# Spectral results of both signs in one store, sent one a step, in a fused attention and spectral-filter kernel

## The chip, the cores and the metric

The kernel runs on one core of one Trainium2 chip. The metric is the device time of one execution in microseconds (us). One execution was also recorded by the hardware profiler; its times are used wherever a single operation is priced.

## What is computed

The reference runs a convolutional-attention hybrid of two layers on x of shape (2, 128, 64, 64), in float32.

- Layer 0: group norm, then neighbourhood attention over 7x7 windows with four heads, two small dense layers with layer norms, and residuals.
- Layer 1, first half: the image as 4096 tokens of 128 features, layer norm, and full self-attention in which queries, keys and values are the same tokens and the diagonal is masked.
- Layer 1, second half: layer norm, then a spectral filter. Sixteen filters are convolved causally with the tokens by FFT, for the sequence as it is and for the sequence with alternating signs; the results are mixed by 128x128 matrices. Four branches of different length are combined by weights that in effect pick one branch. Three short lags of the sequence are added.

Cut to what matters here:

```python
t = _to_tokens(x)
t = t + _L1_attn_ref(_ln_t(t))          # softmax(q q^T / sqrt(128)), diagonal masked
t = t + _L1_ffn_ref(_ln_t(t), ...)      # the spectral filter
...
Uf_p = jnp.fft.rfft(u, n=n, axis=1)
Uf_m = jnp.fft.rfft(u * sgn3, n=n, axis=1)
U_plus  = jnp.fft.irfft(Vf[None, :, :, None] * Uf_p[:, :, None, :], n=n, axis=1)[:, :sl]
U_minus = jnp.fft.irfft(Vf[None, :, :, None] * Uf_m[:, :, None, :], n=n, axis=1)[:, :sl]
out = einsum('btkd,k,kde->bte', U_plus, s, Mpp) + einsum('btkd,k,kde->bte', U_minus, s, Mpm)
```

## The kernel before, in words

The program has four stretches. From 0 to about 350 us it computes layer 0. From 350 to about 770 us it computes the self-attention of batch 0, from 770 to about 1220 that of batch 1. From about 1220 to 1290 it finishes the last forward transforms and the short lags. From there on it runs the filter network for both batches: bursts of small matmuls make products of transformed tokens and filters (line 1570), these are projected by the mixing matrices (line 1589), and inverse transforms come in between (lines 1628 and 1670).

**Attention.** The tokens of a batch form 8 chunks of 512. `attention` walks the 36 pairs of chunks (a, c) with c >= a, four steps a pair. In a step TensorE multiplies keys with queries into a bank (line 927), ScalarE takes the exponential into a tile `e` (line 932, or 943 on the diagonal), and TensorE multiplies the exponentials with the tokens (`other`, line 1057). The same exponentials are needed transposed for the other chunk of the pair. A pair away from the diagonal sends them to DRAM with one 1 MB store issued by ScalarE (`eb`, line 959), SyncE fetches them back in blocks two steps later with four loads of 256 KB (`et`, line 966), VectorE turns 32x32 blocks in place (line 975), and TensorE uses them a few steps later (`own`, line 985). Within batch 1, and in batch 0 from the point where a tile exists, the order of each engine's queue is the order in which the program was written.

**The filler.** Each step of `attention` ends with one call of `fill()`. It first calls `stores()`, then advances one generator by one piece: one from the list `urgent` if there is one, or else one from the list `steps`. A generator that yields None ends the call; one that yields True passes the call on to the other list. `urgent` holds a chain `after(b, c)` for each chunk whose attention is complete, and the short lags. `steps` holds background work: for batch 0 the end of layer 0, the branch weights, the transforms of the filters (`filters`) and the tokens of batch 1; for batch 1 what was left over, and then `for_ffn`, which opens the memory of the network, mixes the 2 x 16 matrices of the four branches (`filter_matrices`), loads the inverse table `inv` (320 KB, SyncE, line 1502), scales it on VectorE (line 1504), and loads the first four sets of blocks and inputs (`load_blocks`).

**A chain.** `after` transposes the attention result of a chunk, divides by the denominator, adds the residual, normalizes (statistics, then apply), and makes the forward transform: 160 bins, of which a row tile holds 128 (real and imaginary part one after the other) and a left-over tile 32. For each of these three parts the function `store` copies two PSUM banks to SBUF (`uo`, ScalarE, line 1141, two buffers), forms sum and difference (`ub`, GpSimd, line 1144, four buffers; VectorE at the very end), and leaves DRAM stores to be issued: for a row tile one of 128 KB for each sign and each of two banks, for the left-over tile one of 32 KB for each sign, bank and half. A chain thus makes 8 large and 8 small stores, and there are 16 chains.

**The stores.** They go to the DRAM array `us`, and those of the filters to `gs` (through the same tag `ub` of four buffers). `store` only appends to the list `fresh_`. Each call of `stores()` issues on ScalarE's queue (line 1095) all that was appended up to the call before the last:

```python
def stores():
    for to, src in behind_:
        nc.scalar.dma_start(out=to, in_=src)
    behind_[:] = fresh_
    fresh_.clear()
```

In the network `inputs` loads from `us` (SyncE, line 1470, 128 KB, one load a burst, 160 in all), and `blocks` loads from `gs` (SyncE, line 1462, four loads a burst). Four bursts are loaded ahead. TensorE's order there is fixed by hand; a burst comes every 4.32 us.

Of the kernel before, what the change touches and what calls it, by code (L numbers as in the profile page):

```python
# [14 lines left out]
P = 128  # L15
# [87 lines left out]
def kernel(  # L103
# [767 lines left out]
    left_row, left_col = Q // P * P, 2 * (Q // P) * P  # L871


    us = dram.tile([Q, 2, 2, SG, FB, NB, 2, P], F32, name="us")
    gs = dram.tile([Q, 2, 2, SG, GROW], F32, name="gs")

    with ap_:
# [208 lines left out]

        spare = [tok[0][:, 0:4, :]]
        adder = [nc.gpsimd]
        behind_ = []

        fresh_ = []

        def stores():
            for to, src in behind_:
                nc.scalar.dma_start(out=to, in_=src)  # L1095
            behind_[:] = fresh_
            fresh_.clear()


        def after(b, c):  # L1100
# [36 lines left out]
            def store(pu, n, r0, m, ri):  # L1137

                for s in range(2):
                    both = sp.tile([P, 512], F32, tag="uo", name="uo", bufs=2)  # L1140
                    nc.scalar.copy(both[:, 0 : 2 * n], pu[s][:, 0 : 2 * n])  # L1141
                    ub = sp.tile([P, 2, 256], F32, tag="ub", name="ub", bufs=4)
                    for sgn, op in enumerate((ALU.add, ALU.subtract)):
                        adder[0].tensor_tensor(ub[:, sgn, 0:n], both[:, 0:n], both[:, n : 2 * n], op)  # L1144
                    for sgn in range(2):
                        to = us[r0 : r0 + m, sgn, :, 2 * hh + s, 2 * fp : 2 * fp + 2, b, par, :]
                        if ri is not None:
                            fresh_.append((to[:, ri], ub[:, sgn, :].rearrange("p (f d) -> p f d", d=P)))
                            continue
                        for f in range(2):  # L1150
                            fresh_.append((to[:, :, f].rearrange("k i d -> i k d"), ub[64 * f : 64 * f + 64, sgn, 0:P]))

            for r0, c0 in row_tiles:
                for ri in range(2):
                    pu = [bank() for _ in range(2)]
                    for e in range(2):
                        for s in range(2):
                            rows_ = slice(s * 64, (s + 1) * 64)
                            nc.tensor.matmul(  # L1159
                                pu[s][:, e * 256 : (e + 1) * 256], lhsT=tr[rows_, hh, e, c0 + ri * P : c0 + (ri + 1) * P],  # L1160
                                rhs=z[rows_, 2 * e : 2 * e + 2, :].rearrange("p f d -> p (f d)"), start=True, stop=True,
                            )
                    store(pu, 256, r0, P, ri)
                    if FB == 4 or ri:
                        yield

            pu = [bank() for _ in range(2)]
            for e in range(2):
# [6 lines left out]
                        )  # L1175
            store(pu, P, left_row, 32, None)
            yield

            if borrowed:
                spare.append(None)  # L1180
# [139 lines left out]
        def filters():  # L1320
# [24 lines left out]
            def store(src, r0, n, ri, s, i, o):  # L1345
                to = bass.AP(
                    gs.tensor, gs.offset + r0 * 4 * SG * GROW + (i * SG + s) * GROW + o * LL,
                    [[4 * SG * GROW, n], [2 * SG * GROW, 2], [1, LL]],
                )
                fresh_.append((to, src))  # L1350

            everything = [(r0, c0 + ri * P, (ri,), P) for r0, c0 in row_tiles for ri in range(2)]
            everything.append((left_row, left_col, (0, 1), 64))
            for r0, c0, parts_, m in everything:
                places = cm[1][:, SG * LL : (3 * SG) * LL].rearrange("p (j e c) -> p j e c", j=SG, e=2)
                for j in range(SG):
                    hh, a = divmod(j, 2)
                    if a == 0:
                        pf = [bank() for _ in range(2)]
                        for e in range(2):  # L1360
                            for s in range(2):
                                rows_ = slice(s * 64, (s + 1) * 64)
                                nc.tensor.matmul(
                                    pf[s][0:m, e * LL : (e + 1) * LL], lhsT=tr[rows_, hh, e, c0 : c0 + m],
                                    rhs=ph[hh, e][rows_].rearrange("p l f k -> p (l f k)"), start=True, stop=True,
                                )
                    sums = places[:, j]
                    whole, before = (places[:, i].rearrange("p e c -> p (e c)") for i in (j, max(j - 1, 0)))
                    if j == 0:
                        nc.scalar.copy(whole[0:m], pf[a][0:m, 0 : 2 * LL])  # L1370
                    else:
                        nc.vector.tensor_tensor(whole[0:m], pf[a][0:m, 0 : 2 * LL], before[0:m], ALU.add)
                    fb = sp.tile([P, 2, LL], F32, tag="ub", name="fb", bufs=4)
                    for sgn, op in enumerate((ALU.add, ALU.subtract)):
                        nc.gpsimd.tensor_tensor(fb[0:m, sgn, :], sums[0:m, 0, :], sums[0:m, 1, :], op)
                    n = m // len(parts_)
                    s = SG - 1 - j
                    for at, ri in enumerate(parts_):
                        mine = slice(at * n, (at + 1) * n)
                        store(fb[mine], r0, n, ri, s, 0, ri)  # L1380
                        if ri == 0:
                            store(fb[mine], r0, n, ri, s, 1, 1)
                    if 1 in parts_:
                        mine = slice(m - n, m)
                        fn = sp.tile([P, 2, LL], F32, tag="ub", name="fn", bufs=4)
# [9 lines left out]
        def filler(b, steps, kept=None):  # L1395

            urgent, done = [], []

            def fill(c=None):
                if c is not None:  # L1400
# [66 lines left out]
        def inputs(b, q):  # L1467

            ut = utp.tile([P, 2, P], F32, tag="ut", name="ut")
            nc.sync.dma_start(  # L1470
                out=ut.rearrange("p s d -> p (s d)"),
                in_=us[2 * q : 2 * q + 2, :, :, :, :, b].rearrange("g n i r f s d -> (g n i r f) (s d)"),
            )
# [11 lines left out]
        def for_ffn():  # L1485
# [9 lines left out]
            inv = l1.tile([P, K2 // BC * 4 + 1, CQ], F32, name="inv")  # L1495
            ctp = ctx.enter_context(tc.tile_pool(name="blocks", bufs=5))
            nc.gpsimd.tensor_copy(mu1, mu)
            with tc.tile_pool(name="mix", bufs=2) as mixp:
                yield from filter_matrices(mpl, mmi, mixp)
            utp = ctx.enter_context(tc.tile_pool(name="inputs", bufs=4))  # L1500

            nc.sync.dma_start(out=inv, in_=nc.inline_tensor(t_out, "t_out").ap().rearrange("(a p) c -> p a c", p=P))
            for s, (lo, hi) in enumerate(((0, CQ // 8), (CQ // 8, CQ // 4), (CQ // 4, CQ // 2), (CQ // 2, CQ))):
                nc.vector.tensor_scalar(inv[:, :, lo:hi], inv[:, :, lo:hi], seg[:, s : s + 1], None, ALU.mult)
            yield
# [355 lines left out]
```

## Time and profile before

| | |
|---|---|
| runs | 2048.33, 2054.34, 2054.42 us; median 2054.34 |
| profiled execution | 2047.53 us, span 2045.8 us, mean granted TensorE clock 0.975 |
| busy in the span | PE 1928.6 us (94%), DVE 942.2 (46%), ACT 728.9 (36%), POOL 598.2 (29%) |
| DMA | 225.97 MB in 262,698 packets; queue 1 (SyncE) 202,050 packets, 127.18 MB; queue 10 (ScalarE) 57,022 packets, 84.26 MB |
| stores to `us` | 128 of 128 KB and 128 of 32 KB, all from ScalarE |
| loads from `us` | 160 of 128 KB, all from SyncE |

PE is TensorE's matmul, PEld its weight load, DVE is VectorE, ACT is ScalarE, POOL is GpSimd, SP is SyncE; ACTq and SPq are the issues of transfers on those engines' queues. "Idle before" is the time that an engine stood before an instruction, and the releaser is what ended it. An instruction stands in the queue of its engine behind all that was written before it, so a wait of one is a wait of all behind it. The granted clock is the share of full speed that TensorE was given.

### The profile page before, as it was taken

The page shows a single profiled execution, that of the slowest core. Times are in us where ns is not written, and L with a number is a line of the kernel's source. Part 1 is how long each engine was busy: PE and PEld are TensorE (multiplying, and loading weights), DVE is VectorE, ACT ScalarE, POOL GpSimd, SP SyncE. Part 2 cuts the span into 40 slices and gives each one's busy share as a digit, 9 for nine tenths or more (in the row PEclk, how much of TensorE's full clock was granted, in tenths as well). Part 3 has the DMA queues.
Part 4 walks back from the last instruction along what each step waited for, and adds up shares of the span by engine and source line. Part 5 has one row for each costly group of instructions (what it writes and reads, how often), then busy time and mean ns, then how long its engine had stood idle before and what let it go on. Part 6 is the DMA issues. An engine that isn't in the chain of part 4 may idle for free. (4 is left out here: it accounts for less than half of the span.)

```text
span 2045.8 us, 50912 instructions
## 1 busy us (share of the span) xinstructions
PE 1928.6 (94%) x20504; PEld 1361.0 (67%) x20504; DVE 942.2 (46%) x2918; ACT 728.9 (36%) x1718; POOL 598.2 (29%) x990
## 2 busy tenths in 40 slices
PE   6899998999998999998987997999999999999998
PEld 4577775444444444443433444999999999999987
DVE  5799996453544344343452345333333333333332
ACT  3788885322222223222231322222222322222222
POOL 4467887303422113103311120122221122222211
PEclk8999999999999999999998997999999999999999
DMA  4222221667656534648765622222222223222211
GB/s 152 62 62 60 62 60 40 189 147 247 183 151 190 148 110 147 177 134 238 225 191 148 179 76 79 74 66 68 65 68 57 52 75 85 68 66 68 65 42 43
DMA packets 262698, 225.97 MB, mean 110 GB/s; under 512 B 122607, under 2 KB 223615, under 8 KB 255040
## 3 DMA queue, kind: packets, MB, share of 16 engines
q1 hardware_dynamic: 202050, 127.18, 25.5%
q10 hardware_dynamic: 57022, 84.26, 11.5%
q0 software_dynamic: 3392, 11.27, 2.0%
q8 instruction: 163, 2.67, 0.5%
q14 instruction: 71, 0.58, 0.1%
HBM read 131.40 MB, written 91.25 MB: 109 GB/s over the span
## 5 line engine op out<-in xcount | busy, mean ns | idle before, releaser
L1575 DVE COPY y<-pc 128x512 f32<-128x512 f32 x320 | 206.2, 686 | 348.2 <-PE pc L1570 347.9
L1589 PE MATMUL acc<-y,mpl 32*128 32x256 f32 x5120 | 324.6, 381 | 0.8 <-DVE af L1599 0.8
L1589 PE MATMUL acc<-y,mmi 32*128 32x256 f32 x5120 | 315.5, 375 | 0.0
L1575 ACT COPY y<-pc 128x512 f32<-128x512 f32 x320 | 171.8, 589 | 393.0 <-PE pc L1570 388.1
L1589 PEld LDWEIGHTS acc<-y,mpl 32*128 32x128 f32 x5120 | 290.1, 186 | 7.9 <-DVE af L1599 1.8
L1589 PEld LDWEIGHTS acc<-y,mmi 32*128 32x128 f32 x5120 | 291.0, 185 | 2.9
L985 PE MATMUL own<-et,tok 128*128 128x512 f32 x448 | 221.3, 618 | 28.7 <-DVE et L975 23.6
L1057 PE MATMUL other<-e,tok 128*128 128x512 f32 x448 | 234.0, 604 | 6.7 <-DVE xa L1066 6.5
L932 ACT ACTIVATE e<-bank 128x512 f32<-128x512 f32 x216 | 127.7, 600 | 283.2 <-PE bank L927 229.4
L927 PE MATMUL bank<-cm 128*128 128x512 f32 x432 | 224.7, 602 | 1.1 <-ACT xa L1192 1.1
L1600 POOL TENSOR_TENSOR af<-af 128x512 f32<-128x512 f32 x39 | 49.7, 1275 | 599.0 <-DVE af L1599 599.0
L1570 PE MATMUL pc<-ct,ut 32*128 32x256 f32 x2560 | 210.9, 378 | 2.1 <-DVE y L1575 2.1
L985 PEld LDWEIGHTS own<-et,tok 128*128 128x128 f32 x448 | 85.7, 196 | 142.8 <-issue 101.2
L1570 PEld LDWEIGHTS pc<-ct,ut 32*128 32x128 f32 x2560 | 172.2, 187 | 8.0 <-DVE y L1575 4.2
L975 DVE STREAM_TRANSPOSE et<-et 128x1024 f32<-128x1024 f32 x108 | 127.7, 1220 | 75.9 <-DMA et<-eb 67.9
L1144 POOL TENSOR_TENSOR ub<-uo 128x256 f32<-128x256 f32 (+1 forms) x160 | 97.1, 638 | 183.1 <-ACT uo L1141 157.7
L1057 PEld LDWEIGHTS other<-e,tok 128*128 128x128 f32 x448 | 82.4, 194 | 99.5 <-issue 81.6
L174 POOL TENSOR_TENSOR ln_rs<-ln_rs,mhalf 128x4 f32<-128x4 f32 x24 | 25.4, 1056 | 346.4 <-DVE ln_rs L173 346.4
L927 PEld LDWEIGHTS bank<-cm 128*128 128x128 f32 x432 | 75.7, 191 | 73.2 <-issue 64.8
L546 ACT ACTIVATE p<-p,mn 128x196 f32<-128x196 f32 x256 | 114.4, 449 | 14.3 <-DVE mn L536 13.8
L1141 ACT COPY uo<-bank 128x512 f32<-128x512 f32 (+1 forms) x96 | 45.6, 517 | 126.0 <-PE bank L1159 85.1
L943 ACT ACTIVATE e<-bank 128x512 f32<-128x512 f32 (+1 forms) x72 | 32.4, 456 | 132.6 <-DVE bank L941 91.8
(264 smaller groups left out, 2596.8 us busy)
## 6 DMA issues: line engine op xcount, KB each, us to landing
eb<-e ACTq DMA_DIRECT2D x54, 1024.0 KB
et<-eb SPq DMA_DIRECT2D x216, 256.0 KB
ut<-us SPq DMA_DIRECT2D x160, 128.0 KB
us<-ub ACTq DMA_DIRECT2D x128, 128.0 KB
ct<-gs SPq DMA_DIRECT2D x320, 40.0 KB
vw<-vd SPq DMA_DIRECT2D x256, 49.0 KB
ct<-gs SPq DMA_DIRECT2D x320, 32.0 KB
vd<-v SPq DMA_DIRECT2D x128, 32.0 KB
```

Of the source, the lines that this page charges most:

```text
L546: nc.scalar.activation(p, p, AF.Exp, bias=t[name + "mn"][:, h : h + 1], scale=-1.0, accum_out=t["den"][:, u, h : h + 1],)
L927: nc.tensor.matmul(ps.rearrange("p (q t j) -> p q t j", q=4, t=4), lhsT=cm[b][:, n * P : (n + 1) * P], rhs=keys.rearrange("p (t q j) -> p ...
L932: nc.scalar.activation(e, ps.rearrange("p (q r) -> p q r", q=4), AF.Exp, bias=0.0, scale=ASCALE)
L975: in_place(nc.vector.transpose(flat, flat))
L985: nc.tensor.matmul(out_, lhsT=tok[b][:, n, :], rhs=e, start=first, stop=last, skip_group_check=True)
L1057: nc.tensor.matmul(turn(other, "p (q r) -> p q r"), lhsT=tok[b][:, n, :], rhs=es[j], start=(j == 0), stop=(j == 3),)
L1141: nc.scalar.copy(both[:, 0 : 2 * n], pu[s][:, 0 : 2 * n])
L1144: adder[0].tensor_tensor(ub[:, sgn, 0:n], both[:, 0:n], both[:, n : 2 * n], op)
L1570: nc.tensor.matmul(pcs[j].rearrange("p (g o c) -> p o g c", g=4, o=2)[:, :, at], lhsT=ut[rows_, par, :], rhs=cv_[rows_], start=True, stop= ...
L1575: (nc.scalar.copy if j % 2 else nc.vector.tensor_copy)(y[:, :, :, 4 * kl + j, :], pcs[j].rearrange("p (g x k) -> p k g x", g=4, k=KF))
L1589: nc.tensor.matmul(acc[j][:, 0:256], lhsT=(mmi if l else mpl)[rows_, k, :], rhs=y[rows_, k, 2 * l : 2 * l + 2].rearrange("p s n x -> p (s ...
L1600: eng.tensor_tensor(af[:, 0:2], af[:, 0:2], af[:, 2:4], ALU.add)
```

## The change

- The array `us` is reordered: batch and token parity come first, the two halves of the frequency pair and the features come last. The two columns of a bank are then neighbours in DRAM, and for a row tile one store carries both signs: 128 partitions x 2 signs x 1 KB, where there were two stores of 128 partitions x 2 x 512 B. A load of `us` now gathers 128 partitions x 2 x 512 B, where it read 1 KB in one run.
- Stores wait in one queue, `queued_`. A call of `stores()` sends one, or two when more than three wait, and none younger than two calls. `room()` is called before each new buffer of the tag `ub`; it sends the oldest ones until no more than three buffers wait. `stores_left()` sends the rest at the end.
- Each of the three forward parts of a chain ends its call as before, and, if fewer than two chains are under way, passes one further call to the background.
- The inverse table is loaded from GpSimd's queue when the network's memory is opened, ahead of the mixing of matrices; the scaling stays where it was.
- `load_blocks` takes two calls for each set, one for the blocks and one for the inputs.

```diff
-    us = dram.tile([Q, 2, 2, SG, FB, NB, 2, P], F32, name="us")
+    us = dram.tile([NB, 2, Q, 2, 2, SG, FB, P], F32, name="us")
...
-        behind_ = []
-
-        fresh_ = []
+        queued_, turns_, crowd_ = [], [0, 0], [[]]
+
+        def send_one():
+            _, _, to, part = queued_.pop(0)
+            nc.scalar.dma_start(out=to, in_=part)
 
         def stores():
-            for to, src in behind_:
-                nc.scalar.dma_start(out=to, in_=src)
-            behind_[:] = fresh_
-            fresh_.clear()
+            turns_[0] += 1
+            for _ in range(1 + (len(queued_) > 3)):
+                if queued_ and queued_[0][0] + 2 <= turns_[0]:
+                    send_one()
+
+        def room():
+
+            while len({n for _, n, _, _ in queued_}) > 3:
+                send_one()
+            turns_[1] += 1
+
+        def fresh(to, part):
+            queued_.append((turns_[0], turns_[1], to, part))
...
+                    room()
                     ub = sp.tile([P, 2, 256], F32, tag="ub", name="ub", bufs=4)
                     for sgn, op in enumerate((ALU.add, ALU.subtract)):
                         adder[0].tensor_tensor(ub[:, sgn, 0:n], both[:, 0:n], both[:, n : 2 * n], op)
+                    to = us[b, par, r0 : r0 + m, :, :, 2 * hh + s, 2 * fp : 2 * fp + 2]
+                    if ri is not None:
+                        fresh(to[:, :, ri].rearrange("k g f d -> k g (f d)"), ub)
+                        continue
                     for sgn in range(2):
-                        to = us[r0 : r0 + m, sgn, :, 2 * hh + s, 2 * fp : 2 * fp + 2, b, par, :]
-                        if ri is not None:
-                            fresh_.append((to[:, ri], ub[:, sgn, :].rearrange("p (f d) -> p f d", d=P)))
-                            continue
                         for f in range(2):
-                            fresh_.append((to[:, :, f].rearrange("k i d -> i k d"), ub[64 * f : 64 * f + 64, sgn, 0:P]))
+                            fresh(to[:, sgn, :, f].rearrange("k i d -> i k d"), ub[64 * f : 64 * f + 64, sgn, 0:P])
...
                     store(pu, 256, r0, P, ri)
-                    if FB == 4 or ri:
-                        yield
+                    yield
+                    if len(crowd_[0]) < 2:
+                        yield True
...
-                in_=us[2 * q : 2 * q + 2, :, :, :, :, b].rearrange("g n i r f s d -> (g n i r f) (s d)"),
+                in_=us[b, :, 2 * q : 2 * q + 2].rearrange("s g n i r f d -> (g n i r f) s d"),
...
-                first_blocks.append((blocks(q), inputs(0, q)))
+                ct = blocks(q)
+                yield
+                first_blocks.append((ct, inputs(0, q)))
                 yield
...
             nc.gpsimd.tensor_copy(mu1, mu)
+            nc.gpsimd.dma_start(out=inv, in_=nc.inline_tensor(t_out, "t_out").ap().rearrange("(a p) c -> p a c", p=P))
             with tc.tile_pool(name="mix", bufs=2) as mixp:
                 yield from filter_matrices(mpl, mmi, mixp)
...
-            nc.sync.dma_start(out=inv, in_=nc.inline_tensor(t_out, "t_out").ap().rearrange("(a p) c -> p a c", p=P))
...
         adder[:] = [nc.vector]
+        crowd_[0] = [None, None]
...
-        for _ in range(2):
-            stores()
+        stores_left()
```

The filter transforms use `room()` and `fresh()` in the same way, and the left-over part of a chain has the same two lines after its `store` as the row tiles.

More of the change, by code (lines that the diff above doesn't have):

```diff
@@ L1088, with stores_left @@
         adder = [nc.gpsimd]
-        behind_ = []
-        fresh_ = []
+        queued_, turns_, crowd_ = [], [0, 0], [[]]
+        def send_one():
+            _, _, to, part = queued_.pop(0)
+            nc.scalar.dma_start(out=to, in_=part)
         def stores():
-            for to, src in behind_:
-                nc.scalar.dma_start(out=to, in_=src)
-            behind_[:] = fresh_
-            fresh_.clear()
+            turns_[0] += 1
[8 more added lines that the diff above has]
+            queued_.append((turns_[0], turns_[1], to, part))
+        def stores_left():
+            while queued_:
+                send_one()
         def after(b, c):
@@ L1177, in after @@
             yield
+            if len(crowd_[0]) < 2:
+                yield True
             if borrowed:
@@ L1349, in store @@
                 )
-                fresh_.append((to, src))
+                fresh(to, src)
             everything = [(r0, c0 + ri * P, (ri,), P) for r0, c0 in row_tiles for ri in range(2)]
@@ L1372, in filters @@
                         nc.vector.tensor_tensor(whole[0:m], pf[a][0:m, 0 : 2 * LL], before[0:m], ALU.add)
+                    room()
                     fb = sp.tile([P, 2, LL], F32, tag="ub", name="fb", bufs=4)
@@ L1384, in filters @@
                         mine = slice(m - n, m)
+                        room()
                         fn = sp.tile([P, 2, LL], F32, tag="ub", name="fn", bufs=4)
@@ L1397, in filler @@
             urgent, done = [], []
+            crowd_[0] = urgent
             def fill(c=None):
@@ L1470, in inputs @@
             nc.sync.dma_start(
-                out=ut.rearrange("p s d -> p (s d)"),
-                in_=us[2 * q : 2 * q + 2, :, :, :, :, b].rearrange("g n i r f s d -> (g n i r f) (s d)"),
+                out=ut,
+                in_=us[b, :, 2 * q : 2 * q + 2].rearrange("s g n i r f d -> (g n i r f) s d"),
             )
```

## The prediction

> **What bounds the kernel now.** I first read the busy time by engine in stretches of the span: the two attention batches (350 to 1220 us), the tail between attention and the filter network (1220 to 1290), and the network itself (1290 to the end).
>
> ```profile
> 350.00:1220.00 870.00, 813.19 (x2526) 379.44 (x2527) 365.34 (x915) 239.24 (x461) 202.41 (x289) 0.97 0.60 169
> 1220.00:1290.00 70.00, 55.66 (x335) 32.83 (x337) 35.17 (x125) 19.47 (x35) 4.91 (x6) 0.85 0.26 73
> 1290.00:2046.00 756.00, 741.55 (x13134) 719.88 (x13126) 256.23 (x456) 207.64 (x418) 165.73 (x390) 0.99 0.24 64
> ```
>
> The columns after the stretch are its length, the busy time of PE, PEld, DVE, ACT and POOL, then the granted clock, the DMA share and GB/s. TensorE is the bound everywhere. In the network it is busy 741.6 of 756 us at clock 0.99: nothing but fewer matmuls helps there. In attention it idles 56.8 us, and a clock of 0.97 costs up to another 26 us (0.03 x 870). In the tail it idles 14.3 us. So the change can win only in the first two stretches.
>
> Next, the line that issues the stores, and who waits for it:
>
> ```profile
> L1095 ACTq DMA_DIRECT2D us<-ub x256: 361/503/3100, 480.1 to 1266.1; - x128
> L1095 ACTq DMA_DIRECT2D gs<-fb x24: 520/606/1686, 494.9 to 531.5; - x24
>   ACT e L932: 36.2, 6
>   ACT e L943: 29.2, 5
>   ACT xa L1192: 19.9, 3
>   ACT uo L1141: 19.5, 9
> ```
>
> Minimum, median and maximum are in ns. A store holds ScalarE's queue for 0.5 us as a rule and for up to 3.1 us at worst, and the exponentials of attention (e, L932 and L943) stand behind it. Then the ACT part of the timeline at one such place, what PE made of it, and the clock in the five microseconds there:
>
> ```profile
> 1097.16 9.18 ACTq L1095 DMA_DIRECT2D us<-ub  x8
> 1106.39 0.98 ACT L943 ACTIVATE e<-bank 128x512 f32<-128x512 f32 x2 [9.73 <-DMA us<-ub]
> 1107.04 0.48 PE L949 MATMUL bank<-ident,e 128*128 128x128 f32 x1 [4.67 <-ACT e L943]
> 1105.00:1110.00 5.00, 2.96 (x6) 1.64 (x7) 0.29 (x1) 0.98 (x2) 0.00 (x0) 0.50 0.38 101
> ```
>
> Eight stores in one step keep ScalarE 9.18 us, the exponential comes 9.73 us late, PE stands for 4.67 us and goes on at half clock. The second kind of stall is on DVE and PE:
>
> ```profile
> 1068.29 1.11 DVE L191 TENSOR_SCALAR z<-tt,ln_mv,ln_rs 128x128 f32<-128x128 f32 x4
> 1077.60 0.98 DVE L1504 TENSOR_SCALAR inv<-inv,seg 128x80 f32<-128x80 f32 x4 [8.21 <-DMA inv<-t_out]
> 1080.91 2.08 PE L985 MATMUL own<-et,tok 128*128 128x512 f32 x2 [7.09 <-DVE et L975]
> ```
>
> DVE scales the inverse table right after its load was issued (SP, at 1070.85), waits 8.21 us, and the transposes of attention wait behind it.
>
> [...]every gap of 4.6 us or more is followed by slices at 0.50 to 0.55, and so is one of 3.52 us (0.53). [...]the slow stores fall where SP moves the exponentials (et<-eb, 256 KB each).[...]
>
> **The change part by part.** A *turn* is one call of the filler (144 in a batch's pair loop, some 2.7 us apart).
>
> *Both signs in one store.* 128 stores of 128 KB become 64 of 256 KB; each keeps 256 runs, now of 1 KB. The same shape is in the trace: gs<-fb, 128 partitions x 2 x 1 KB, minimum 0.520 us, beside a median of 0.503 for today's stores. So 64 issues x 0.503 = 32 us less on ACT's queue. The 128 small stores (32 KB, some 0.4 to 0.55 us) stay. Queue 10 carries 16,384 fewer packets.
>
> *One store a turn.* Today a chain's 16 stores leave in turns of 4, 4 and 8. Counting the new code by turns, an isolated chain sends 1, 1, 1, 1, 2, 2, 2, 1, 1; the filter part still sends up to 4 in a few turns, because the limit of three waiting buffers forces them out. ACT is then held 0.5 to 1.1 us a turn where it was held 4.5 to 13.3. ACT is busy 239 of 870 us, so that fits. What it unblocks, by PE's gaps in the timeline: 2.89 us at 588, 3.52 at 659, 1.09 at 846, 0.70 + 1.64 + 2.95 at 1032 to 1041, 4.67 at 1107: together 17.5. The 5 us slices around these show 0.96, 0.70, 0.79, 0.53, 0.51, 0.80, 0.50 and 0.82, a deficit of 2.39 x 5 = 12 us, of which I count 9, since some of it lies inside the gaps. Sum 26.5, of which I take 85%: **22.5**. The gap of 5.57 at 958 (with 2 for the clock) came from late moves whose source was sent by ACT between two bunches (931.84 to 945); DMA load has a part in it, so half: **3.8**. The two gaps of 2.43 at 523 and 528 (with 1.7 for the clock) belong to the filter stores, partly waiting for POOL's results, which stay: 30% of 6.6, **2.0**.
>
> *Held buffers.* Buffers of ub stay unsent longer, but a chain's fifth buffer is asked for four turns after the first instead of two, so POOL's 13.4 us of waiting for us<-ub shrinks if anything; POOL works 202 of 870 us. Bounds: -2 to +5 us; I take 0.
>
> *Forward steps spaced.* Three turns more for each chain that is alone (13 instead of 10), given to the background. Counted through, each batch ends with the same work left over (two whole chains, the rest of a third, the lags), so the tail does not grow. Weight mixing starts three turns later (some 8 us) and ended 90 us early; cover remains. Cost 0; a chain pushed into the tail would cost 5.
>
> *Inverse table early, on POOL.* The 320 KB load leaves SP's queue (0.38 us) and goes to POOL's (0.75 us by the st rows), some 50 turns before it is used. It stands in front of the first st loads of 256 KB; POOL already waits there for the same released memory (the copy of mu). Gap 7.09 and 1.8 for the clock, 90%: **8.0**.
>
> *Load blocks split in two turns.* SP's issues of 2.5 to 4.5 us no longer stand in one piece before the moves. No PE gap hangs on it: 0.
>
> *Loads of us.* 160 loads of 128 KB go from 128 runs of 1 KB to 256 of 512 B. SP in the steady network:
>
> ```profile
> 1451.64 0.33 SPq L1470 DMA_DIRECT2D ut<-us  x1
> 1452.01 3.22 SPq L1462 DMA_DIRECT2D ct<-gs  x4
> 1455.96 0.33 SPq L1470 DMA_DIRECT2D ut<-us  x1
> 1456.33 2.45 SPq L1462 DMA_DIRECT2D ct<-gs  x4
> ```
>
> A burst comes every 4.32 us and SP needs 2.8 to 3.6 of it. At the price of the store of that very shape (0.503) it needs 0.17 more. Packets: 160 x 128 = 20,480 at queue 1's mean of 41 ns (25.5% of 16 x 2045.8 us over 202,050) is at most 52 us over 16 engines, so the share rises from 0.24 to at most 0.31. Four bursts of prefetch (17 us) hide it: 0. With the batch outermost, reads of batch 0 no longer overlap batch 1's writes (SP once waited 80.3 us for them); that wait ended at 1275, before PE needed the data: 0.
>
> *Tail.* Gaps of 1.45 (1256) and 3.16 (1267) follow bunches of 8 and 12 stores; the new flush still has six small ones: half of 4.6, **2.3**. The gaps of 4.29 and 2.06 hang on DVE's serial chain and stay.
>
> Sum: 22.5 + 3.8 + 2.0 + 8.0 + 2.3 = 38.6 us; less 5 for new short waits where a store now meets an exponential: **33**. The profiled execution took 2047.53 us (span 2045.8), so 2014.5. The median shown, 2054.34, is 6.8 above it, and two of three runs lie there, which would give 2021. I say **2018**.
>
> **Rivals.**
> *DMA is the limit in the dense part.* The share is 0.78 to 0.83 between 900 and 1050 us, and the bytes stay; the late moves would then stay late and only the table and the pure ACT stalls (659, 1107) would come back: 8.0 + 3.5 + 4.7 = 16 us, 2031 to 2038, and up to 2043 if the table helps less. Against it: at 1080 to 1085 the share is 0.02, and between 1105 and 1110 only 0.38, while PE stands.
> *Nothing comes of it.* The queue sends two a turn whenever more than three wait[...]: the same waits, cut in pieces, hit as many exponentials. Then only the table's 8 us come, and new short stalls eat them: 2050 to 2056.
> *Slower, by SP in the network.* If the load of 256 runs takes over 1.87 us to issue (4.32 less 2.45 for the four block loads; today it takes 0.33), SP and no longer PE sets the burst. At 2.5 us the burst is 4.95 us, and 156 x 0.63 = 98 us more: 2120. For it: stores of that shape took up to 3.10. Against it: [...]here the share is 0.24.
>
> **How the numbers follow.** Stalls go: 0.70. DMA limit: 0.18. Nothing: 0.06. Slower: 0.06. A measurement of this kernel tells 0.3%, some 6 us, from no change; the first two are faster by more, so faster 0.88, same 0.06, slower 0.06. All the priced stalls together are 54 us (26.5 + 7.5 + 6.6 + 8.9 + 4.6), which from 2051 gives 1997 as the low end; the DMA rival's weak end gives 2043.
>
> **What would show it.** Right: 192 issues of us<-ub with no run of more than two outside the filter part, no wait of e for us<-ub over 3 us, no wait of inv, PE idle in attention down from 57 to some 30 us and the clock up to 0.98 or more, the network's 756 us unchanged. Wrong: waits of DVE for et<-eb above today's 67.9 us, waits of PE for y or ut in the network, waits of POOL for us<-ub above 20 us, or a tail longer than 70 us.

## The result, and the profile after

The changed kernel takes 2020.16 us in the median of five runs (2016.05 to 2021.44), beside 2048.91 us (2046.07 to 2054.42) for the kernel before. The ratio is 0.9849, with a 95% interval from 0.9827 to 0.9871: about 31 us faster by the ratio, 28.8 between the two medians. The profiled execution has a span of 2018.4 us, 27.4 less than before (2045.8).

Where the 27.4 us came from can be read from four marks in the timeline. The first diagonal product of attention (line 936) starts 0.4 us earlier than before. From there to the end of the last `own` product 853.3 us pass instead of 875.4: 22.0 less. From that point to the first burst of the network 47.0 pass instead of 50.8: 3.7 less. The rest is 1.2 less. So the gain is in attention, and a little in the tail. By kind it is 16.9 us less idle time of PE (100.3 instead of 117.2 in the whole span) and 10.5 us less busy time (1918.1 instead of 1928.6) for the same 20,504 matmuls, at a mean granted clock of 0.982 instead of 0.975. The same stretches as in the prediction (length, busy time of PE, PEld, DVE, ACT and POOL, granted clock, DMA share, GB/s):

```profile
350.00:1200.00 850.00, 807.43 (x2535) 377.90 (x2536) 368.50 (x920) 243.61 (x460) 203.19 (x289) 0.99 0.61 173
1200.00:1270.00 70.00, 58.05 (x418) 35.66 (x420) 35.19 (x123) 20.74 (x38) 4.90 (x6) 0.88 0.26 81
1270.00:2018.00 748.00, 734.52 (x13042) 713.58 (x13034) 254.88 (x454) 206.45 (x416) 165.77 (x390) 0.99 0.24 64
```

PE's idle time in attention fell from 56.8 to 42.6 us, and the clock rose from 0.97 to 0.99. The issues of stores (minimum, median and maximum in ns) and those who waited for them:

```profile
L1093 ACTq DMA_DIRECT2D us<-ub x192: 490/521/3307, 480.7 to 1239.7; - x192
  ACT e L932: 7.2, 2
  ACT e L943: 7.0, 2
  ACT xa L1211: 4.9, 1
```

There are 192 issues, as counted beforehand, with about the median of before (0.521 us, 0.503 before), though each large store now carries twice the bytes. The exponentials waited 65.4 us for line 1095 before; now they wait 14.2, of which 5.39 are a single wait at 935.90. `uo` no longer stands in the list. The table, first its issue on POOL and then its first use on DVE:

```profile
L1522 POOL DMA_DIRECT2D inv<-t_out x1: 960/960/960, 923.9 to 923.9; - x1
1079.84 0.26 DVE L1528 TENSOR_SCALAR inv<-inv,seg 128x80 f32<-128x80 f32 x1
```

There is no wait in front of the scaling. SP in the steady network:

```profile
1430.67 0.37 SPq L1492 DMA_DIRECT2D ut<-us  x1
1431.08 2.46 SPq L1484 DMA_DIRECT2D ct<-gs  x4
```

A load with twice the runs costs 0.37 us of issuing instead of 0.33. Lastly, what is left. These lines are from ACT's, DVE's and PE's timeline, with one five-microsecond window between them:

```profile
930.54 2.73 ACTq L959 DMA_DIRECT2D eb<-e  x1
944.54 2.37 DVE L975 STREAM_TRANSPOSE et<-et 128x1024 f32<-128x1024 f32 x2 [9.90 <-DMA et<-eb]
946.96 3.78 PE L985 MATMUL own<-et,tok 128*128 128x512 f32 x4 [6.66 <-DVE et L975]
945.00:950.00 5.00, 3.04 (x4) 1.49 (x5) 3.80 (x5) 0.00 (x0) 1.49 (x2) 0.50 0.95 309
1013.41 5.48 ACTq L1093 DMA_DIRECT2D us<-ub  x2
1019.32 3.31 ACTq L1093 DMA_DIRECT2D us<-ub  x1
1022.70 2.23 ACTq L1093 DMA_DIRECT2D us<-ub  x1
1028.52 2.37 DVE L975 STREAM_TRANSPOSE et<-et 128x1024 f32<-128x1024 f32 x2 [4.51 <-DMA et<-eb]
1030.94 3.78 PE L985 MATMUL own<-et,tok 128*128 128x512 f32 x4 [4.34 <-DVE et L975]
```

The two large gaps of the dense part are still there (5.57 at 958 and 2.95 at 1041 before). In both, the moved exponentials arrived late: DVE waits for them, and PE for DVE. The DMA share in the five-microsecond windows from 925 to 940 is 0.90, 1.02 and 0.98, and 0.95 right behind the first gap (1 is all engines busy; the view can give a little more). ScalarE was not free in front of them either. The 1 MB store at 930.54 took 2.73 us to issue, where none took over 0.38 before, and four small stores at 1013 to 1025 held ScalarE for 11.0 us. These lines alone don't tell which of the two made the moves late; the run with the recut stores, below, tells more.

### The profile page after: what moved, and what is told of

Its sections match the earlier page's. It is cut to its first block, busy times and chain, and to the rows that moved or that the text cites. A ratio compares the mean times of both kernels' runs of the same rounds, so it can differ in the third digit from the quotient of the medians.

```text
span 2018.4 us, 50825 instructions
## 1 busy us (share of the span) xinstructions
PE 1918.1 (95%) x20504; PEld 1355.7 (67%) x20504; DVE 944.1 (47%) x2918; ACT 733.5 (36%) x1718; POOL 599.5 (30%) x991
## 4 chain that ended last, share of the span: by engine, by line
PE 53%; DVE 3%; DMA 3%; issue 1%; POOL 1%; SPq 0%; ACT 0%; ACTq 0%; DVEq 0%; POOLq 0%
PE acc L1613 28%; PE pc L1594 7%; PE own L985 6%; PE bank L927 4%; PE other L1057 3%; PE bank L1221 1%; DMA us<-ub 1%; DMA et<-eb 1%; PE pc L1652 1%; PE bank L1175 1%; PE bank L936 1%; DVE et L975 1%; PE pc L1665 0%; PE pc L1694 0%; PE bank L202 0%
## 5 line engine op out<-in xcount | busy, mean ns | idle before, releaser
L927 PEld LDWEIGHTS bank<-cm 128*128 128x128 f32 x432 | 76.4, 191 | 74.4 <-issue 67.9
L546 ACT ACTIVATE p<-p,mn 128x196 f32<-128x196 f32 x256 | 114.4, 449 | 14.5 <-DVE mn L536 13.9
L536 DVE CUSTOM_DVE_ANT_0 p<-bank,tab 128x196 f32<-128x196 f32 x256 | 76.7, 357 | 4.9 <-PE bank L523 4.7
```

The source lines that it names most:

```text
L536: nc.vector.tensor_tensor_reduce(t[name + "p"][:, h, :], t[name + "S"][h][:, 0:KEYS], tab[:, ci, h, :], 1.0, 3.0e38, ALU.add, ALU.min, t[n ...
L546: nc.scalar.activation(p, p, AF.Exp, bias=t[name + "mn"][:, h : h + 1], scale=-1.0, accum_out=t["den"][:, u, h : h + 1],)
L927: nc.tensor.matmul(ps.rearrange("p (q t j) -> p q t j", q=4, t=4), lhsT=cm[b][:, n * P : (n + 1) * P], rhs=keys.rearrange("p (t q j) -> p ...
```

## The experiments

All ratios are to the kernel before, run on the same chip in turn with it, with 95% intervals. One per cent is some 20 us.

**One part alone on the kernel before**

*The table early.*

```diff
             nc.gpsimd.tensor_copy(mu1, mu)
+            nc.gpsimd.dma_start(out=inv, in_=...t_out...)
...
-            nc.sync.dma_start(out=inv, in_=...t_out...)
```

> The kernel before with one part of the change: the inverse table is loaded from GpSimd's queue when the network's memory is opened; all else as before. Theory (the parts add, and each stall goes where its cause goes): the wait of 8.21 us of DVE for inv and the PE gap of 7.09 us at 1081 go, with about 1.8 us for the half clock after it; 8 us faster, ratio 0.996. Rival (DMA is the limit in the dense part): the early load of 320 KB falls into the dense stretch at about 930 us and delays a move there; the late gap goes, an earlier one grows by 2 to 5 us, and 3 to 6 us are left, ratio 0.997 to 0.9985.

Measured: 0.9953 (0.9941 to 0.9966), about 9.6 us. The gap of 7.09 us is gone. In the dense part PE's gap is 5.12 us, beside 5.57 before:

```profile
961.59 3.59 PE L985 MATMUL own<-et,tok 128*128 128x512 f32 x4 [5.12 <-DVE et L975]
```

So the early load costs nothing there on this kernel, and the theory's 8 us hold.

*The array and both signs in one store, bunches as before.*

```diff
-    us = dram.tile([Q, 2, 2, SG, FB, NB, 2, P], F32, name="us")
+    us = dram.tile([NB, 2, Q, 2, 2, SG, FB, P], F32, name="us")
...
+                    if ri is not None:
+                        fresh_.append((to[:, :, ri].rearrange("k g f d -> k g (f d)"), ub))
+                        continue
```

> The kernel before with one part of the change: the reordered array and both signs in one store of 256 KB, bunches as before (2, 2 and 8 stores in three steps instead of 4, 4 and 8). Theory (the bunch of eight small stores is the trouble, and the large ones add little): ACT saves 32 us of issuing spread over 870 us, PE's gaps at 588, 659, 1032 to 1041 and 1107 stay for the most part; 3 to 6 us faster, ratio 0.997 to 0.9985. Rival (the number of packets matters): queue 10 carries 16,384 packets fewer and the moves come earlier, 10 us or more faster, ratio under 0.995. In the network the loads of two runs of 512 B cost nothing by both.

Measured: 0.9915 (0.9897 to 0.9933), 17 us, and the rival was right on the size. The PE gaps behind the stores shrank without any spacing: 2.89 to 2.08 at 588, 3.52 to 1.76 at 659, and 1.09 at 846 to under 0.8. Whether it was the number of issues or of packets, this run doesn't separate. PE's idle time in the whole span is nearly that of before, 115.1 us instead of 117.2; the profiled execution is 10.5 us shorter, and 8.4 of them are busy time, at a mean granted clock of 0.979 instead of 0.975.

*The queue alone.* Old array, 256 stores, late table, close steps; `room`, `fresh` and `stores_left` as in the change.

```diff
         def stores():
-            for to, src in behind_:
-                nc.scalar.dma_start(out=to, in_=src)
-            behind_[:] = fresh_
-            fresh_.clear()
+            turns_[0] += 1
+            for _ in range(1 + (len(queued_) > 3)):
+                if queued_ and queued_[0][0] + 2 <= turns_[0]:
+                    send_one()
...
```

> The kernel before with one part of the change: the queue (one store a turn, two when more than three wait, room before each buffer); old array, 256 stores, table loaded late, steps close. Every version with the queue so far lies at 2016 to 2020 us, whichever other part was taken out. Theory (the queue alone frees ScalarE and reaches the same floor, the other parts are worth something only without it): ratio 0.985 to 0.988, at most the late table's wait on top. Rival (any two parts reach the floor, none alone): the queue alone gives what the array gave, ratio 0.990 to 0.993.

Measured: 0.9924 (0.9906 to 0.9942), 16 us, as the rival said. The waits of the exponentials for `us` fell to 1.9 us, and of the gaps at 588, 659, 846 and 1107 only one of 3.06 us near the last is left. GpSimd's waits for a free buffer rose from 13.4 to 34.9 us. PE's idle time is 115.2 us, nearly that of before, and 14.5 of the 16.5 us between the two profiled executions are busy time: the gaps at those places have gone but for that one, the clock from 350 to 900 us is 1.00 instead of 0.98, and idle time has come back elsewhere. The table's gap is there in full:

```profile
1068.04 3.78 PE L985 MATMUL own<-et,tok 128*128 128x512 f32 x4 [6.99 <-DVE et L975]
```

*The small stores cut another way.*

```diff
-                            fresh_.append((to[:, :, f].rearrange("k i d -> i k d"), ub[64 * f : 64 * f + 64, sgn, 0:P]))
+                            i = sgn
+                            fresh_.append((us[r0 : r0 + m, :, i, 2 * hh + s, 2 * fp + f, b, par, :], ub[64 * f + 32 * i : 64 * f + 32 * i + 32, :, 0:P]))
```

> The kernel before with only the small stores of the left-over tile cut another way: instead of one store of 32 KB for each sign and column (destination indexed real/imaginary part first, then bin, then feature), one of 32 KB for each part and column, with bins first and both signs in it. As many stores, as many bytes, the bunches as before.[...] Theory A[...]: issues of the eight small ones no longer grow to over 1 us each, the waits of e for us<-ub fall from 57 us (31.9 + 25.5) to under 20, and the time falls by 10 to 20 us, ratio 0.990 to 0.995. Theory B (it is the number of issues in one step[...], whatever the form): no change within 4 us, ratio 0.998 to 1.002.

Measured: 0.9956 (0.9939 to 0.9973), 9 us; the interval overlaps theory A's. A's other signs came in part. Of the 128 small stores 9 took over 1 us to issue, where 24 did before, and the longest fell from 3.10 to 2.35 us; but the waits of `e` for `us<-ub` fell only to 41.6 us (22.5 + 19.1), not under 20. The same cut on the changed kernel gave nothing (below). Why the new form has fewer long issues, and why it helps alone, no run shows.

*The stores on GpSimd's queue.*

```diff
-                nc.scalar.dma_start(out=to, in_=src)
+                nc.gpsimd.dma_start(out=to, in_=src)
```

> The kernel before with the stores of us and gs issued from GpSimd's queue instead of ScalarE's; bytes, forms, bunches and the step in which they are sent stay. Theory (the time is lost because ScalarE's queue is held): PE's gaps behind late exponentials (523, 528, 659, 846, 1032 to 1041, 1107) go, as far as the moves are not late by themselves; 15 to 25 us faster, ratio 0.988 to 0.993, unless GpSimd, [...]becomes late with ub. Rival (DMA is the limit): the late moves stay, and no more than 8 us come back, ratio 0.996 or more.

Measured: 1.0156 (1.0134 to 1.0178), slower, and much as in the theory's exception GpSimd became late, though not with `ub` first. No exponential waits for a store any more, but the power function of the layer norm, which GpSimd computes, stands behind the filter stores, and PE behind it. From POOL's and PE's timeline:

```profile
560.05 1.04 POOL L174 TENSOR_TENSOR ln_rs<-ln_rs,mhalf 128x4 f32<-128x4 f32 x1
561.62 1.15 PE L202 MATMUL bank<-ident,tok 128*128 128x128 f32 x4 [19.68 <-DVE tok L191]
985.56 3.78 PE L985 MATMUL own<-et,tok 128*128 128x512 f32 x4 [7.71 <-DVE et L975]
```

The last line is no test of the first gap of the dense part, though it stands at its place. There DVE stood 14.46 us for a mixing load (`mpl` for `st`), with the transposes behind it; that load was issued on GpSimd's queue, at 977.17, among the stores. DVE's waits for the moves themselves (`et<-eb`) fell from 67.9 to 30.1 us; the kernel is slower, so the moves also have more time.

**One part taken out of the changed kernel**

*Bunches again.*

```diff
-            for _ in range(1 + (len(queued_) > 3)):
-                if queued_ and queued_[0][0] + 2 <= turns_[0]:
-                    send_one()
+            while queued_ and queued_[0][0] + 2 <= turns_[0]:
+                send_one()
```

> The changed kernel with stores sent in bunches again (all that are two turns old); array, both signs, spacing and early table as changed. Theory (the queue is what counts): bunches of up to eight small stores hold ScalarE again, the waits of e for us<-ub come back to over 20 us, 8 to 14 us slower than the changed kernel, ratio 0.989 to 0.992. Rival (the array, the spacing and the table reach the floor without the queue): the single gains on the kernel before, 17 us for the array and 9.6 for the table, add up to 26, ratio 0.986 to 0.988.

Measured: 0.9912 (0.9896 to 0.9929), wholly above the changed kernel's interval; 13 us of the gain hang on the queue. The exponentials wait 36.9 us for `us` again, and PE with them:

```profile
1097.11 0.48 PE L949 MATMUL bank<-ident,e 128*128 128x128 f32 x1 [4.76 <-ACT e L943]
```

*The old array, with the queue.* The reading of `ut` and the stores go back to the old form:

```diff
-    us = dram.tile([NB, 2, Q, 2, 2, SG, FB, P], F32, name="us")
+    us = dram.tile([Q, 2, 2, SG, FB, NB, 2, P], F32, name="us")
...
-                        fresh(to[:, :, ri].rearrange("k g f d -> k g (f d)"), ub)
+                            fresh(to[:, ri], ub[:, sgn, :].rearrange("p (f d) -> p f d", d=P))
```

> The changed kernel with the array us in its old order, so that each sign and bank has a store of its own again (256 stores, large ones of 128 KB in runs of 512 B) and loads read 1 KB in one run; queue, spacing and table as changed. Theory from the sum in the prediction (the queue carries most): 5 to 8 us slower than the changed kernel, 2025 to 2028. Rival, since the reordered array alone gave 17 us on the kernel before (fewer packets and issues carry most): 12 to 18 us slower, 2032 to 2038. A chain then has 16 stores to send at one or two a turn.

Measured: 0.9854 (0.9839 to 0.9869), no different from the changed kernel. Both theories fell: the array gives 17 us alone, where stores leave in bunches, and nothing that can be told beside the queue and the other parts.

*The table late, with the rest.*

```diff
             nc.gpsimd.tensor_copy(mu1, mu)
-            nc.gpsimd.dma_start(out=inv, in_=...t_out...)
...
+            nc.sync.dma_start(out=inv, in_=...t_out...)
```

> The changed kernel with the inverse table loaded late again, from SyncE's queue just ahead of its scaling. Theory (the parts add): the wait of DVE for inv of some 8 us and the PE gap of some 7 us at about 1070 come back, 8 to 10 us slower than the changed kernel, about 2029. Rival (the early load costs a delayed move in the dense stretch): PE's gap of 6.66 us at 947 shrinks to 3 or less, and the whole is only 3 to 6 us slower than the changed kernel, about 2025.

Measured: 0.9835 (0.9813 to 0.9857), not slower. The theory fell, and the rival is not shown either: the gap at 947 is 4.85 us beside 6.66, but the intervals overlap. What happened to the table's wait is plain in SP's and DVE's timeline:

```profile
1076.71 0.38 SPq L1526 DMA_DIRECT2D inv<-t_out  x1
1079.73 0.44 DVE L1528 TENSOR_SCALAR inv<-inv,seg 128x80 f32<-128x80 f32 x2 [0.60 <-DMA inv<-t_out]
```

Here the load lands in 3 us instead of 7, and DVE reaches the scaling only then. The array alone does not do that (a gap of 7.06 us is left at 1075), nor does the queue alone (6.99). Whether the spacing of the steps does, or only several parts together, was not separated.

*The steps close again.* These two lines go in both places where they stand:

```diff
-                    if len(crowd_[0]) < 2:
-                        yield True
```

> The changed kernel without the extra calls between a chain's forward steps, so that a chain that is alone makes its three parts in three following turns again; the queue, the array and the table as changed. Theory (the queue spaces the stores, and the spacing of the steps adds little): within 4 us of the changed kernel, 2016 to 2024. Rival (with the steps close, the fifth buffer is asked for two turns after the first, GpSimd waits for it and copies back up on ACT): 5 to 8 us slower, 2025 to 2028.

Measured: 0.9857 (0.9837 to 0.9876), no difference that can be told, as the theory said. GpSimd's waits for a free buffer rose from 6.6 to 20.6 us, as the rival expected, but PE lost nothing by it. The second call of `load_blocks` stayed in this run; no run takes it out.

*The small stores recut, on the changed kernel.*

```diff
-                    for sgn in range(2):
+                    for i in range(2):
...
-                            fresh(to[:, sgn, :, f].rearrange("k i d -> i k d"), ub[64 * f : 64 * f + 64, sgn, 0:P])
+                            fresh(to[:, :, i, f], ub[64 * f + 32 * i : 64 * f + 32 * i + 32, :, 0:P])
```

> The changed kernel with the small stores of the left-over tile cut by part and column, both signs in each[...]; as many and as large as before. Theory A[...]: issues of over 2 us on ACT become rare, the largest falls from 3.3 us to under 1.5, eb leaves ACT earlier, and the gaps at 947 and 1031 (6.66 and 4.34) shrink; 5 to 8 us faster than the changed kernel, 2012 to 2015. Theory B (one store a turn already took what there was to take): within 3 us of it, 2017 to 2023.

Measured: 0.9856 (0.9841 to 0.9871). Theory B holds. The longest issue did fall to 1.65 us, but the gaps at 945 and 1030 are 6.27 and 7.23 us. From 928 to 1021 us the 1 MB stores now take 0.33 us to issue and no store to `us` over 1.3, and still the moves are late. PE's line and the windows in front of it, with the DMA share in the last column but one:

```profile
1029.97 3.62 PE L985 MATMUL own<-et,tok 128*128 128x512 f32 x4 [7.23 <-DVE et L975]
1020.00:1025.00 5.00, 2.74 (x13) 1.36 (x11) 0.98 (x3) 0.38 (x1) 0.98 (x2) 1.00 1.06 323
1025.00:1030.00 5.00, 0.03 (x1) 0.03 (x1) 2.45 (x3) 0.00 (x0) 0.00 (x0) 0.65 1.05 218
```

Shorter issues on ScalarE did not bring those moves forward here; the DMA share just ahead of PE's start was 1.06 and 1.05.

**The dense part by itself**

*The mixing pauses while stores wait.*

```diff
-                yield from filter_matrices(mpl, mmi, mixp)
+                for _ in filter_matrices(mpl, mmi, mixp):
+                    yield
+                    for _ in range(12):
+                        if not queued_:
+                            break
+                        yield True
```

> The changed kernel with one addition: while stores of a chain wait in the queue, the mixing of matrices pauses (up to 12 turns each time), so that its loads of 256 KB do not fall beside the stores. Theory (the gaps of 6.66 us at 947 and 4.34 at 1031 are late moves in the densest stretch of DMA, where chain stores, mixing loads, the table and the moves of attention meet): both gaps fall under 2 us, DVE's wait for et<-eb falls from 82 us to under 65, 8 to 14 us faster than the changed kernel, 2006 to 2012. Rival (the moves and the attention's own 1 MB stores fill the engines by themselves): the gaps stay, within 4 us of the changed kernel, or up to 6 us slower where the postponed block loads come late.

Measured: 0.9771 (0.9755 to 0.9787), a median of 2002.2 us: below both kernels, by the ratios some 16 us faster than the changed one. PE in the stretch from 900 to 1060 us, first the changed kernel and then this one:

```profile
900.00:1060.00 160.00, 143.80 (x396) 64.29 (x395) 73.19 (x131) 44.50 (x92) 42.57 (x60) 0.96 0.78 220
900.00:1060.00 160.00, 152.14 (x433) 68.50 (x431) 67.76 (x121) 46.34 (x91) 43.00 (x61) 0.98 0.81 227
```

PE is idle 7.9 us there instead of 16.2. The gap at 1031 is gone, that at 1120 too, and one of 4.36 us at 939 stays (mean clock 0.86 from 925 to 950). The mean DMA share is not lower, 0.81 beside 0.78, so the mean did not tell here when a move is late; that what stands beside it at its moment does is my reading, not shown. Two signs failed: the first gap did not fall under 2 us, and DVE's waits for `et<-eb` are still 78.2 us. The edit does more than pause. The mixing now runs until the end of attention (the table is scaled at 1178), and the block loads of `gs` were placed earlier on SP's queue, from 948 us on. How much each of these gives was not separated.

*The first step waits too.* The edit above, and the same pause ahead of the table and the first three mixing loads:

```diff
+            for _ in range(12):
+                if not queued_:
+                    break
+                yield True
```

> The version with the pause, which also waits with the first step of the network's work (the table of 320 KB and the first three mixing loads of 256 KB) until the first chain's stores of batch 1 have left. Theory (the one large gap left, 4.36 us at 939 with half clock after it, comes from those loads standing beside the chain's stores): it falls under 2 us, 4 to 7 us faster than the version with the pause, ratio 0.9735 to 0.9755. Rival (stores and moves alone make it late, or the postponed work runs past the end of attention and is paid in the tail): within 3 us of the version with the pause or slower, ratio 0.976 to 0.980.

Measured: 0.9757 (0.9734 to 0.9780). That lies between the theory and the rival, and cannot be told from the version above. The gap at 939 did close, and one of the same size stands earlier. From DVE's and PE's timeline:

```profile
925.17 0.98 DVE L1537 TENSOR_SCALAR inv<-inv,seg 128x80 f32<-128x80 f32 x4 [11.22 <-DMA inv<-t_out]
928.47 3.78 PE L985 MATMUL own<-et,tok 128*128 128x512 f32 x4 [4.16 <-DVE et L975]
```

It is not a late move. The pause did not hold the loads back: GpSimd issued the table at 918.17 and the first mixing loads from 919.13 on, beside 918.14 and 919.10 in the version above. But in this version the scaling of the table stands ahead of the mixing in VectorE's queue, although the program writes it after; DVE waited 11.22 us for the table there, with the transposes behind it. So the queues did not keep the order of the program here, and this run tests neither the theory nor the rival.

## Why the prediction was right, and where its sum was not

- **The time.** 2018 was forecast and 2020.16 measured, inside the range of 1997 to 2043. In the profiled executions 33 us were forecast and 27.4 came. About 11 of the 38.6 us summed stood for the clock, and busy time fell by 10.5. The shortfall is in the idle time: some 23 us of it were to go, the 5 for new waits taken off, and 16.9 went. The number is near because the two terms that failed, below, are about a quarter of the sum, not because every term held.
- **Where.** Attention and the tail were named; 22.0 and 3.7 of the 27.4 lie there (the tail was put at 2.3). The network kept its time: PE is busy 734.5 of 748 us. The loads of 512 B cost what was said, nothing beyond 0.04 us of issuing each; the DMA share stayed at 0.24.
- **Store stalls, term of 22.5.** The gaps at 588, 659, 846 and 1107 (12.2 us) went, and the run with bunches shows that the queue is the reason: without it 13 us are lost and the waits are back. The part at 1032 to 1041 did not go. Its 5.29 us, with its clock, were counted as a ScalarE stall at 85%; in the changed kernel 7.4 us stand there (0.65 + 1.85 + 0.57 + 4.34). This is the step that failed, and for two reasons. ACT was to be held 0.5 to 1.1 us a turn, and two stores held it 5.48 us there; in this place the rival that expected the same waits cut in pieces had it right. And where the recut stores left it free, 7.23 us of PE's gap remained, beside a DMA share of 1.06 and 1.05.
- **Late move at 958, term of 3.8.** It failed too. The gap is 6.66 us after, 5.51 with the array alone, 7.58 with the queue alone, 6.27 with the recut stores. I took it to be half ScalarE's doing; no run shows that freeing ScalarE brings half of it back. The version with the pause, which spreads the mixing over a longer time, shrank it to 4.36; what in that version did so was not separated. The DMA rival was thus right about the place, and wrong in that it would have left only 16 us: the gap of 2.89 at 588, for one, went too. The prediction argued against it from a slice that it misread. PE stood until 1080.91, and in the five microseconds before 1080, in which it did nothing, the DMA share was 0.84, not 0.02:

```profile
1075.00:1080.00 5.00, 0.00 (x0) 0.00 (x0) 2.40 (x6) 0.00 (x0) 0.00 (x0) 0.77 0.84 275
```

- **Slow stores and the moves.** Nor do the slow stores fall only where SyncE moves exponentials, as the prediction has it. The bunch that it shows at 1097 stands beside SyncE's block loads, issued from 1095.90 on, and six of its eight stores took 6.66 us from 1099.68 on, while the DMA share was 0.49 and then 0.38. Most issues over 1 us were those of small stores: 24 of 29 before.
- **Both signs in one store.** 32 us less of issuing were forecast. The large stores took 62.9 us of it before and 37.2 after: 25.7 less, since one of 256 KB costs a little more than one of 128 KB (0.547 us beside 0.482).
- **Table, term of 8.0.** Alone on the kernel before it gives 9.6 us. In the whole change it is not needed: without it the time is not longer.
- **Sums of parts.** Array, queue and table alone give 0.85, 0.76 and 0.47%, 2.08% together; the change gives 1.51%. What the array gives alone is not missed beside the queue, and the table's wait goes without the early load when the other parts are there. Yet the queue alone stays some 15 us short of the whole, and the array, the table and the spacing can each be left out at no loss. Which of them together make up the 15 us was not tested. The prediction had priced the array at almost nothing by itself, which only the other parts beside it make true. That its 64 saved issues of 0.5 us count where they stand in a row in front of an exponential is my reading, not a result.
- **Filter stores, term of 2.0.** The gaps at 523 and 528 went from 4.86 to 4.05 us: 0.8, and less than said. The limit of three waiting buffers still forces four stores into some turns.
- **Short new waits, 5 us off.** They came: 1.79 + 1.19 at 772 and 777, where a store that itself waits for GpSimd stands in front of the exponentials, and a late move of 3.30 at 1120.
- **Signs.** Of the signs of being right three failed: one exponential waited 5.39 us for a store, not under 3; PE idles 42.6 us in attention, not some 30; and outside the filter part stores still left four in a row at the end of each batch's attention, at 758 and at 1192, and more in the tail. The others came.
- **What was wrong at no cost.** I expected that reads of batch 0 would no longer wait for batch 1's writes. SP still waited 76.8 us for `us<-ub` at that load, until the network began; PE did not need the data sooner. The mark that waits of DVE for `et<-eb` above 67.9 us would mean a wrong forecast was a poor one: they rose to 82.0 while the kernel became faster. That DVE, less held up elsewhere, reaches them sooner is my guess, not shown.

## What to carry to other kernels

Issues on a compute engine's queue held up that engine here: eight stores in one step kept ScalarE 9.18 us, and the exponential queued behind them came 9.73 us late. Spread over the steps they held the exponentials 14.2 us in all, not 65.4, and cost PE little, except in the dense part, where single ones took 2 to 3 us. Parts of a change that cure the same stall do not add up, so take each out of the changed kernel as well as adding it to the old one; of the four parts taken out here only the queue could not be left out. Where a gap survives the freeing of the engine it was blamed on, look at which transfers stand beside the late one: a version that paused the background loads, and thereby also shifted others, was another 16 us faster. And look in the trace whether an edit moved what it was meant to move: the last one here did not.

## What the runs showed of the hardware

The prices by size are medians over the single records of one trace.

- A store of 256 KB in 256 runs of 1 KB took 0.547 us to issue on ScalarE's queue (after), one of 128 KB in 256 runs of 512 B 0.482 (before), and one of 32 KB in 64 runs of 512 B 0.508 in both kernels. The small store was thus no cheaper to issue here than that of 128 KB. A load with 256 runs instead of 128 took 0.366 us instead of 0.326.
- On ScalarE's queue a store to `us` took up to 3.1 us to issue before, 3.3 after, and 6.5 at worst in the run with the queue alone. From GpSimd's queue the same 256 stores took 0.661 to 0.835 us each, with no long ones. The other work in GpSimd's queue paid for it: PE waited 19.68 us at 561 for a chain that had stood behind the filter stores there.
- Before, a gap of 2.89 us of PE was followed by a slice at clock 0.70, and one of 3.52 us by one at 0.53. After, a gap of 3.30 us at 1120 was followed by a slice at 1.00. So the length of a gap alone did not decide the clock after it in these traces. What the prediction says of gaps of 4.6 us or more holds for those of attention (4.67, 5.57 and 7.09 us, with slices at 0.50, 0.50 and 0.55); the first matmul of the program, after 10.98 us, was followed by slices at 1.00.
